# Column maxima brought together on VectorE, one running sum over eight key tiles in the first attention phase, and LayerNorm of the first tiles two ahead of the transposes

## The chip, the cores and the metric

The kernel runs on one core of one Trainium2 chip. The metric is the device time of one execution in microseconds (us), as the median of several runs. Five engines work at the same time, each taking its own instructions strictly in the order in which they were issued: TensorE (PE: matrix products, and transposes by way of an identity matrix; PEld is its loading of weights), VectorE (DVE), ScalarE (ACT), GpSimd (POOL) and SyncE (SP, which here only issues transfers). Semaphores tie them together.

## The reference

One block of a transformer with LayerNorm ahead of each half, in fp32: `x` is [2, 1024, 1024] (batch, tokens, features), there are 32 heads of 32 features, and the hidden width of the second half is 2752.

```python
def attention(x):
    qkv = x @ qkvw + qkvb                      # 1024 -> 3 * 1024
    q, k, v = heads(qkv)                       # [2, 32, 1024, 32] each
    probs = softmax(q @ k.T / sqrt(32))
    return (probs @ v) @ ow + ob

def ffn(x):
    return (silu(x @ W_gate.T) * (x @ W_up.T)) @ W_down.T   # 1024 -> 2752 -> 1024

x = x + attention(layernorm(x))
x = x + ffn(layernorm(x))
```

## The kernel before, in words

**Phases and units.** Attention is done in four phases (2 batches x 2 blocks of 512 queries). A phase has 16 units, and a unit is two heads against 512 queries, that is, 1024 columns. The keys of a unit come in 8 tiles of 128 (`kt` 0 to 7). For each pair of tiles PE computes the transposed scores (`scores`, L510) into two PSUM tiles `s` of 128 keys x 1024 columns; ACT copies each to an SBUF tile `p` (`keep`, L529), and DVE keeps the running maximum over the key tiles in `top` (`largest`, L526).

**The maximum of a column** has then still to be taken over 128 partitions. `maximum` does it in steps that are put off by set delays: two halves, each a transposition of 32x32 blocks on DVE (L549) and a reduction into 16 columns of `part` (L550), at 4600 and 6400 ns; then `turn`, at 10500 ns. In `turn` PE transposes `part` as a whole (L564) into a PSUM tile, and DVE reduces that over its four groups of 32 into `neg`, with the sign changed (L565). `neg` goes to memory at 12000 ns, and comes back spread over all partitions as `m` at 14500 ns (L573).

**Exponentials and sums.** `less_maximum` adds `m` to a tile `p` (POOL, L580; in phase 0 the tiles with `kt % 4 == 3` go to DVE), 3500 ns later ACT takes the exponential (L589), and `add` (L603) adds neighbouring tiles, so that the column of ones that gives the softmax denominator has to be multiplied with fewer tiles. In phase 0 every fourth tile holds the sum of four tiles: tile 1 and tile 5 get one addition, tile 3 and tile 7 two (by 1 and by 2 back). In the other phases every second tile holds the sum of two. `differences` (POOL, L594 and L597) takes differences of the value tiles, so that the products with summed tiles still come out as the plain sum. `values` (L618) multiplies a tile `p` by its values, four products of 32 columns side by side, and, where `summed(kt)` says so, by the ones; in phase 0 that is at `kt` 3 and 7. All of it goes into the PSUM tile `acc`.

**The order of the work** is written out in the program, not found by a scheduler. An `Emitter` merges a list of attention steps (`paced`, one beat per key tile) with a list of other work (`fill`), by a clock that adds up set costs; `later(delay, fn)` puts a step off until that clock has moved on by the delay, and a step can need a mark (`needs=("added", k, kt)`) that another has given. In phase 0, the fill is the projections of q, k (L370) and v (L432) for both batches; in phases 1 to 3 it is output projection (L780), second LayerNorm and feed-forward part of the block before (L922 gate and up products, L1071 down products), and phase 3 is followed by that of the last block alone. On every engine the instructions run in the order in which this merging put them. Projections, transposes, gate, up and down products, and `turn`, all draw their PSUM tile from one pool of three (`lps`); a new tile waits until the tile three before it has been read out. The tiles `p` are a ring of 19.

**The head.** Before phase 0, the first four tiles of 128 tokens are loaded, normed (`norm`, DVE statistics L237 to L246, ACT scaling L247) and transposed on PE (L258) through the same three PSUM tiles, with the read-out of the first half of a tile on DVE (L264) and the second on ACT (L266). `ln_steps` issues the norm of the tile `ahead` places further on before the transposes of the present one; here `ahead` is 1.

Of the kernel before, what the change touches and what calls it, by code (L numbers as in the profile page):

```python
# [9 lines left out]
F32 = mybir.dt.float32  # L10
F32R = mybir.dt.float32r
AF = mybir.ActivationFunctionType
ALU = mybir.AluOpType
AX = mybir.AxisListType

P = 128
HEADS = 32
HD = 32
# [86 lines left out]
def merged(main, side):  # L105

    out, m, n = Steps(), len(main.items), len(side.items)
    for i, step in enumerate(main.items):
        out.items.append(step)
        out.items.extend(side.items[i * n // m : (i + 1) * n // m])  # L110
    return out
# [19 lines left out]
def preln_block_kernel(  # L131
# [14 lines left out]
    nc = tc.nc  # L146
# [3 lines left out]
    NT = S // P  # L150
    NS = S // NH
    NHF = H // NH
    TB = NH // P
# [4 lines left out]
    HPG = P // HD  # L158
# [8 lines left out]
    const = ctx.enter_context(tc.tile_pool(name="const", bufs=1))  # L167
# [29 lines left out]
    def lps(name, shape=(P, NH)):  # L197
        return psum.tile(list(shape), F32, tag="lin", bufs=3, name=name)

    def small(shape, tag, bufs, name):  # L200
        return const.tile(shape, F32, tag=tag, bufs=bufs, name=name)

    ident = const.tile([P, P], F32, tag="ident", name="ident")
# [25 lines left out]
    em = Emitter()  # L229
# [229 lines left out]
    NQ = NH // 2  # L459


    part = const.tile([P, P], F32, tag="part", name="part")
    nc.vector.memset(part, 0.0)

    class Unit:

# [75 lines left out]
        def maximum(self):  # L542

            n = HD // NS
            self.m = att.tile([P, S], F32, tag="m", bufs=2, name=f"m_{self.name}")

            def half(s):
                cols = slice(s * NH, (s + 1) * NH)
                nc.vector.transpose(self.m[:, cols], self.top[:, cols])  # L549
                nc.vector.tensor_reduce(  # L550
                    part[:, s * n : (s + 1) * n],
                    self.m[:, cols].rearrange("p (b j) -> p b j", j=HD),
                    AX.X,
                    ALU.max,
                )

            for s in range(NS):
                em.later(4600.0 + 1800.0 * s, lambda s=s: half(s))
            d2 = dram.tile([S], F32, tag="d2", bufs=3, name=f"d2_{self.name}")
            neg = small([HD, HD], "neg", 1, f"neg_{self.name}")  # L560

            def turn():
                pt = lps(f"top_{self.name}", (P, P))
                nc.tensor.transpose(pt, part, ident)  # L564
                nc.vector.tensor_reduce(  # L565
                    neg, pt[:HD, :].rearrange("b (a i) -> b i a", i=HD), AX.X, ALU.max, negate=True
                )

            em.later(10500.0, turn)
            em.later(12000.0, lambda: nc.sync.dma_start(d2.rearrange("(b i) -> b i", i=HD), neg))  # L570
            em.later(
                14500.0,
                lambda: nc.sync.dma_start(self.m, d2.partition_broadcast(P)),  # L573
                ("max", self.n),
            )

        def less_maximum(self, kt):
            p = self.p[kt]
            eng = nc.vector if self.phase == 0 and kt % 4 == 3 else nc.gpsimd
            eng.tensor_tensor(p, p, self.m, ALU.add)  # L580
            em.later(3500.0, lambda: self.exponential(kt))
            if kt % 2 == 1:
                twice = self.phase == 0 and kt % 4 == 3
                em.later(8100.0, lambda: self.add(kt, 1), None if twice else ("added", self.n, kt))
                if twice:
                    em.later(9900.0, lambda: self.add(kt, 2), ("added", self.n, kt))

        def exponential(self, kt):
            nc.scalar.activation(self.p[kt], self.p[kt], AF.Exp, scale=SCALE)  # L589
# [1 line left out]
        def differences(self):  # L591

            v = self.v.rearrange("p (i a) n -> p i a n", a=2)
            nc.gpsimd.tensor_tensor(v[:, :, 0, :], v[:, :, 0, :], v[:, :, 1, :], ALU.subtract)  # L594
            if self.phase == 0:
                v = self.v.rearrange("p (i a) n -> p i a n", a=4)
                nc.gpsimd.tensor_tensor(v[:, :, 1, :], v[:, :, 1, :], v[:, :, 3, :], ALU.subtract)  # L597

        def add(self, kt, back):


            eng = nc.vector if self.phase == 0 or kt % RUN == RUN - 1 else nc.gpsimd
            eng.tensor_tensor(self.p[kt], self.p[kt], self.p[kt - back], ALU.add)  # L603

        def summed(self, kt):
            return kt % (4 if self.phase == 0 else 2) == (3 if self.phase == 0 else 1)

        def values(self, kt):

# [592 lines left out]
    def joined(qs):  # L1202
        out_ = Steps()
        for k in qs:
            out_.items.extend(k.items)
        return out_

    with tc.manual_schedule():

        head, fill, keep_qk = Steps(), Steps(), Steps()  # L1210

        def two(fn, *args, **kw):

            q = Steps()
            fn(q, *args, **kw)
            return q

        def ln_steps(q, b, t0, t1, tools, ahead):

            load, norm, turn, _ = tools  # L1220
            for t in range(t0, t1):
                if t + ahead < t1:
                    q.add(lambda t=t + ahead: norm(t))
                turn(q, t)
                if t + 5 < NT:
                    q.add(lambda t=t + 5: load(t))

        tools = load, norm, turn, _ = ln1(0)
        for t in range(4):
            head.add(lambda t=t: load(t))  # L1230
        head.add(lambda: nc.sync.dma_start(bqk_t, b_qk))
        for _ in range(4):
            head.add(wst.next)
        head.add(lambda: load(4))
        for _ in range(8):
            head.add(dst.next)
        for _ in range(5):
            head.add(wst.next)
        head.add(lambda: norm(0))
        ln_steps(head, 0, 0, TB, tools, 1)  # L1240
        for _ in range(2):
            head.add(dst.next)
        qk_steps(head, 0, 0, [0])
        head.add(lambda: norm(TB))
        side = two(ln_steps, 0, TB, NT, tools, 1)
        head.items += merged(two(v_steps, 0, 0, range(TB)), side).items
        qk_steps(head, 0, 0, [1])

        v_steps(fill, 0, 0, range(TB, NT))
        for g in range(1, G // 2):  # L1250
            qk_steps(fill, 0, g)
        v_steps(fill, 0, 1)
        for g in range(G // 2, G - 2):
            qk_steps(fill, 0, g)

        tools = load1, norm1, turn1, stats1 = ln1(1)
        for t in range(5):
            fill.add(lambda t=t: load1(t))
        qk_steps(fill, 0, G - 2, [0])
        fill.items += merged(two(qk_steps, 0, G - 1, [0]), stats1(0, TB)).items  # L1260
        last = two(qk_steps, 0, G - 2, [1])
        qk_steps(last, 0, G - 1, [1])
        fill.items += merged(last, two(ln_steps, 1, 0, TB, tools, 1)).items
        fill.items += merged(two(v_steps, 1, 0, range(2)), stats1(TB, TB)).items
        fill.items += merged(
            two(v_steps, 1, 0, range(2, TB)), two(ln_steps, 1, TB, NT, tools, 1)
        ).items
        v_steps(fill, 1, 0, range(TB, NT))
        for g in range(0, G // 2):
            qk_steps(fill, 1, g)  # L1270
        v_steps(fill, 1, 1)
        for g in range(G // 2, G - 2):
            qk_steps(fill, 1, g)
        for s in range(NS):
            for g in range(G - 2, G):
                qk_steps(keep_qk, 1, g, [s])
            if s == 0:
                keep_qk.add(lambda: None, gives=("half", 1))

        def rest(n):  # L1280

            q, late, st = Steps(), Steps(), {}
            b, blk = divmod(n, NS)
            turn = oproj_steps(q, b, blk, st)
            ffn_steps(q, b, blk, st, turn)
            while late.cost < 30 * MM4:
                late.items.insert(0, q.items.pop())
            return q, late


        rests = [rest(n) for n in range(B * NS)]
        lists = attention_steps([(n + 1) * UNITS * NT + 2 * NT for n in range(B * NS - 1)])
        side = [*prep_ctx(0), *prep_ctx(1)]
        em.run(head)
        em.run(fill, lists[0], side=(*side, weight_sum_steps()))
        keep = keep_qk
        for (q, late), beats in zip(rests, [*lists[1:], None]):
            em.run(joined([keep, q]), beats, side=side)
            keep = late
        em.run(keep)  # L1300
        em.settle(True)
# [51 lines left out]
```

## Time and profile before

| | |
|---|---|
| median of 3 runs | 3283.42 us (3279.31 to 3285.41) |
| profiled execution, its own time | 3281.96 us |
| its span, first to last instruction | 3280.2 us |
| mean granted TensorE clock | 0.994 |
| PE busy | 3217.5 us (98%) |
| DVE, ACT, POOL busy | 1920.4, 1431.2, 1758.6 us |
| transposes in `turn` (L564) | 64, together 19.0 us busy |
| reductions in `turn` (L565) | 64, mean 272 ns |
| products with ones (L618) | 1792 instructions, together 137.7 us busy |
| additions of `p` on DVE (L603) | 192, mean 1595 ns |

A line of the profile's list of groups names the source line, the engine, the operation, output and inputs, the shapes, the number of instructions, their busy time together, the mean of one in nanoseconds, and the idle time of the engine just before them with what ended it. Ends of matmuls are modelled, and neighbouring ones overlap, so the busy time of PE is no measure of what an instruction costs there; the distance from one start to the next is. A line of the list of waits names who waited, for whom, the sum in us, the number of times and the longest. Phase 0 lasts from about 120 to 860 us, phase 1 to about 1540, phase 2 to about 2210, phase 3 to about 2770, and the last block's feed-forward part follows.

### The profile page before, as it was taken

How to read it: one execution, taken by the hardware profiler on the slowest of the kernel's cores; microseconds unless marked ns; L12 is line 12 of the kernel's file. 1: busy time of each engine (PE TensorE's matmuls, PEld its weight loads, DVE VectorE, ACT ScalarE, POOL GpSimd, SP SyncE). 2: the span in 40 equal slices, each digit the busy share in tenths (PEclk: the TensorE clock that was granted, in tenths of full speed). 3: DMA queues.
4: the chain of work that ended last, by engine and by line, in shares of the span. 5: the costliest groups of instructions: out<-in, count | busy, mean ns of one | idle time of the engine just before them, and what ended most of it. 6: DMA issues, size and time to landing. Idle time of an engine off the chain costs nothing. (4 is left out here: it accounts for less than half of the span.)

```text
span 3280.2 us, 43732 instructions
## 1 busy us (share of the span) xinstructions
PE 3217.5 (98%) x16320; PEld 1801.1 (55%) x16320; DVE 1920.4 (59%) x2478; ACT 1431.2 (44%) x1570; POOL 1758.6 (54%) x871
## 2 busy tenths in 40 slices
PE   8999999999999999999999999989999999999999
PEld 4444444444347655663466556634655566477775
DVE  2265676666356766666666666676666664344334
ACT  2244554444455545563655455545555554010000
POOL 0267776876676655568665555667765665200000
PEclk9999999999999999999999999999999999999999
DMA  4556766655534445446344444463444444544442
GB/s 155 171 184 193 226 192 203 200 180 161 158 99 135 142 151 146 146 146 200 107 142 145 139 141 137 145 192 110 137 145 146 146 138 140 184 151 153 153 152 97
DMA packets 337826, 507.29 MB, mean 155 GB/s; under 512 B 105424, under 2 KB 122064, under 8 KB 337616
## 3 DMA queue, kind: packets, MB, share of 16 engines
q1 hardware_dynamic: 281424, 405.91, 40.3%
q10 hardware_dynamic: 56192, 98.60, 9.8%
q8 instruction: 130, 2.13, 0.3%
q14 instruction: 80, 0.66, 0.1%
HBM read 429.14 MB, written 75.24 MB: 154 GB/s over the span
## 5 line engine op out<-in xcount | busy, mean ns | idle before, releaser
L580 POOL TENSOR_TENSOR p<-p,m 128x1024 f32<-128x1024 f32 x480 | 1180.8, 2483 | 13.6 <-DMA m<-d 13.4
L529 ACT COPY p<-s 128x1024 f32<-128x1024 f32 x512 | 516.7, 1011 | 872.1 <-DVE top L526 664.5
L526 DVE TENSOR_TENSOR top<-s,top 128x1024 f32<-128x1024 f32 x384 | 468.1, 1219 | 289.0 <-PE s L510 280.0
L589 ACT ACTIVATE p<-p 128x1024 f32<-128x1024 f32 x512 | 532.2, 1057 | 234.7 <-POOL p L580 206.8
L922 PE MATMUL p<-sum,m 128*128 128x256 f32 x2688 | 617.8, 383 | 4.9 <-DVE sum L904 3.3
L603 POOL TENSOR_TENSOR p<-p,p 128x1024 f32<-128x1024 f32 x96 | 227.2, 2367 | 658.9 <-ACT p L589 598.3
L922 PEld LDWEIGHTS p<-sum,m 128*128 128x128 f32 x2688 | 503.2, 190 | 124.7 <-issue 43.0
L922 PE MATMUL p<-xn2T,m 128*128 128x256 f32 x2016 | 473.5, 384 | 1.9 <-ACT gate L934 1.3
L370 PE MATMUL pq<-xnT,wqk 128*128 128x512 f32 x1024 | 463.7, 601 | 0.0
L1071 PE MATMUL pd<-wp,h 128*128 128x512 f32 x960 | 442.3, 607 | 8.3 <-DVE x L1084 6.4
L922 PEld LDWEIGHTS p<-xn2T,m 128*128 128x128 f32 x2016 | 378.2, 191 | 98.5 <-issue 45.4
L603 DVE TENSOR_TENSOR p<-p,p 128x1024 f32<-128x1024 f32 x192 | 306.2, 1595 | 134.1 <-ACT p L589 134.0
L370 PEld LDWEIGHTS pq<-xnT,wqk 128*128 128x128 f32 x1024 | 187.2, 190 | 252.8 <-issue 249.0
L1071 PEld LDWEIGHTS pd<-wp,h 128*128 128x128 f32 x960 | 179.3, 193 | 242.5 <-issue 203.4
L510 PE MATMUL s<-q,k 32*128 32x512 f32 x2048 | 300.8, 645 | 7.1 <-ACT p L529 7.0
L1084 DVE TENSOR_TENSOR x<-pd,x 128x512 f32<-128x512 f32 x360 | 236.9, 681 | 86.8 <-PE pd L1071 86.7
L618 PE MATMUL acc<-p,vals 128*32 128x256 f32 x4096 | 266.0, 383 | 1.8 <-DVE p L603 1.8
L1184 POOL TENSOR_TENSOR ws<-raw 128x512 f32<-128x512 f32 x62 | 93.7, 1512 | 299.9 <-DMA raw<-in_w_gu 170.5
L432 PE MATMUL pvv<-wv,xnT 128*128 128x512 f32 x512 | 233.3, 600 | 1.5 <-ACT xnT L266 1.5
L780 PE MATMUL po<-wo,ctx 128*128 128x512 f32 x512 | 234.6, 607 | 0.0
L618 PEld LDWEIGHTS acc<-p,vals 128*32 128x32 f32 x4096 | 120.1, 110 | 143.6 <-issue 70.2
L950 ACT ACTIVATE gate<-gate 128x512 f32<-128x512 f32 x84 | 52.9, 630 | 278.4 <-DVE gate L949 278.0
(96 smaller groups left out, 2451.3 us busy)
## 6 DMA issues: line engine op xcount, KB each, us to landing
m<-dws SPq DMA_DIRECT2D x336, 256.0 KB
m<-in_w_gu SPq DMA_DIRECT2D x252, 256.0 KB
wp<-ddn SPq DMA_DIRECT2D x160, 256.0 KB
m<-d SPq DMA_DIRECT2D x64, 512.0 KB
wp<-in_w_dn SPq DMA_DIRECT2D x120, 256.0 KB
raw<-in_w_gu ACTq DMA_DIRECT2D x84, 256.0 KB
dws<-ws ACTq DMA_DIRECT2D x84, 256.0 KB
x<-in_x SPq DMA_DIRECT2D x32, 512.0 KB
```

The source lines that it names most:

```text
L370: nc.tensor.matmul(ps, wqk[b, g, w, hk][:, k, :], xnT[b, s][:, kc, :], start=(kc == 0), stop=(kc == KC - 1),)
L510: nc.tensor.matmul(ps[a][:, h * NH : (h + 1) * NH], self.k[rows, i * P : (i + 1) * P], self.q[rows, :], start=True, stop=True,)
L526: nc.vector.tensor_tensor(self.top, s, self.p[0] if kt == 1 else self.top, ALU.max)
L529: nc.scalar.copy(self.p[kt], s)
L580: eng.tensor_tensor(p, p, self.m, ALU.add)
L589: nc.scalar.activation(self.p[kt], self.p[kt], AF.Exp, scale=SCALE)
L603: eng.tensor_tensor(self.p[kt], self.p[kt], self.p[kt - back], ALU.add)
L618: nc.tensor.matmul(self.acc[j * HD : (j + 1) * HD, c : c + NQ], w(h), self.p[kt][:, q0 : q0 + NQ], start=start, stop=stop, skip_group_chec ...
L780: nc.tensor.matmul(st["ps"], ctxT[b, blk][:, g, t * P : (t + 1) * P], st["w"][hf, g], start=(g == 0), stop=(g == G - 1),)
L922: nc.tensor.matmul(ps, mats[c, n][:, kc, :], rhs, start=(kc == 0), stop=(kc == hk - 1),)
L1071: nc.tensor.matmul(st["pd"], lefts[n](pi)[:, j, t * P : (t + 1) * P], st["wp", pi, n, j], start=(j == 0), stop=(j == PART // 2 - 1),)
L1084: nc.vector.tensor_tensor(xs, st["pd"], xs, op)
```

## The change

Three things are changed. `turn` no longer uses PE and PSUM: `part` has 32 columns instead of 128, DVE transposes each of its four 32x32 blocks into `turned` and reduces that; `turn` is due at 8200 instead of 10500 ns. In phase 0 tile 7 gets a third addition (4 back), so that it holds the sum of all eight tiles; the ones are multiplied with tile 7 alone, and POOL takes one more difference of values per unit. In the head, tile 1 is normed before the first transposes, and from there on the norms run two tiles ahead.

```diff
-    part = const.tile([P, P], F32, tag="part", name="part")
-    nc.vector.memset(part, 0.0)
+    part = const.tile([P, HD], F32, tag="part", name="part")
...
+            turned = small([HD, HPG, HD], "turned", 1, f"turned_{self.name}")
             def turn():
-                pt = lps(f"top_{self.name}", (P, P))
-                nc.tensor.transpose(pt, part, ident)
+                for a in range(HPG):
+                    nc.vector.transpose(turned[:, a, :], part[a * HD : (a + 1) * HD, :])
                 nc.vector.tensor_reduce(
-                    neg, pt[:HD, :].rearrange("b (a i) -> b i a", i=HD), AX.X, ALU.max, negate=True
+                    neg, turned.rearrange("b a i -> b i a"), AX.X, ALU.max, negate=True
                 )
-            em.later(10500.0, turn)
+            em.later(8200.0, turn)
...
             if kt % 2 == 1:
-                twice = self.phase == 0 and kt % 4 == 3
-                em.later(8100.0, lambda: self.add(kt, 1), None if twice else ("added", self.n, kt))
-                if twice:
-                    em.later(9900.0, lambda: self.add(kt, 2), ("added", self.n, kt))
+                backs = [b for b in (1, 2, 4) if self.phase == 0 and (kt + 1) % (2 * b) == 0] or [1]
+                for i, back in enumerate(backs):
+                    em.later(
+                        8100.0 + 1800.0 * i,
+                        lambda back=back: self.add(kt, back),
+                        ("added", self.n, kt) if back == backs[-1] else None,
+                    )
...
             if self.phase == 0:
                 v = self.v.rearrange("p (i a) n -> p i a n", a=4)
                 nc.gpsimd.tensor_tensor(v[:, :, 1, :], v[:, :, 1, :], v[:, :, 3, :], ALU.subtract)
+                v = self.v
+                nc.gpsimd.tensor_tensor(v[:, 3, :], v[:, 3, :], v[:, 7, :], ALU.subtract)
...
         def summed(self, kt):
-            return kt % (4 if self.phase == 0 else 2) == (3 if self.phase == 0 else 1)
+            n = NT if self.phase == 0 else 2
+            return kt % n == n - 1
...
         head.add(lambda: norm(0))
-        ln_steps(head, 0, 0, TB, tools, 1)
+        head.add(lambda: norm(1))
+        ln_steps(head, 0, 0, TB, tools, 2)
```

## The prediction

> **What bounds the kernel now.** I read the page's busy times first, then PE's list of waits, the groups by shape, the granted clock around the longest waits, and the timeline at two places.
>
> ```profile
> PE 3217.5 (98%) x16320; PEld 1801.1 (55%) x16320; DVE 1920.4 (59%) x2478; ACT 1431.2 (44%) x1570; POOL 1758.6 (54%) x871
> ```
>
> PE is hardly ever idle, so the time is PE's work plus PE's few waits. What leaves PE counts almost in full; what is put on another engine counts only where PE comes to wait for it. The waits, us in sum, times, longest:
>
> ```profile
> PE top L564 <- DVE part L550: 16.1, 10, 3.0
> PE pt_a L258 <- ACT x L247: 10.2, 4, 7.8
> PE pd L1071 <- DVE x L1084: 7.1, 12, 1.4
> PE s L510 <- ACT p L529: 7.0, 5, 2.6
> ...
> PE top L564 <- DVE xn2T L264: 2.0, 1, 2.0
> PE acc L618 <- DVE p L603: 1.8, 2, 1.5
> ```
>
> The longest entry is the transpose that the change removes: PE reaches it before DVE has reduced `part`, and everything queued on PE behind it stands still. The second entry is the head. The groups that change:
>
> ```profile
> L603 DVE TENSOR_TENSOR p<-p,p 128x1024 f32<-128x1024 f32 x192 | 306.2, 1595 | 134.1 <-ACT p L589 134.0
> ...
> L618 PE MATMUL acc<-p,ones 128*32 128x256 f32 x1792 | 137.7, 379 | 0.0
> ...
> L549 DVE STREAM_TRANSPOSE m<-top 128x512 f32<-128x512 f32 x128 | 89.9, 702 | 1.8
> ...
> L564 PE MATMUL top<-ident,part 128*128 128x128 f32 x64 | 19.0, 297 | 19.0 <-DVE part L550 16.1 <-DVE xn2T L264 2.0 <-DVE x L1084 0.7
> ...
> L565 DVE TENSOR_REDUCE neg<-top 32x32 f32<-32x128 f32 x64 | 17.4, 272 | 38.6 <-PE top L564 38.4
> ```
>
> DVE in turn stood 38.4 us waiting for these transposes. Around one of the long waits (columns: stretch, length, busy of PE, PEld, DVE, ACT, POOL, granted clock, DMA):
>
> ```profile
> 2028.10:2030.80 2.70, 0.02 (x4) 0.00 (x0) 2.67 (x6) 1.01 (x1) 0.00 (x0) 1.00 0.33 97
> ...
> 2032.95:2036.36 3.41, 3.41 (x5) 1.30 (x4) 2.95 (x6) 0.00 (x0) 0.00 (x0) 0.50 0.36 100
> 2036.36:2040.00 3.64, 3.64 (x51) 1.65 (x49) 1.70 (x2) 2.54 (x3) 0.50 (x1) 1.00 0.37 122
> ```
>
> PE idles 2.7 us, and soon after the granted clock is 0.50 for 3.41 us. So a long wait costs twice.
>
> **The compiled order.** The change leaves the order of all other instructions on PE as it was, but for shifts by one product in some places. The sum can therefore be made instruction by instruction, against the profiled execution's 3281.96 us.
>
> **A, the transposes' own time.** Start to next start, a transpose amid products takes 0.109 us (49 of 64), right after scores 0.165 us (15): 5.3 + 2.5 = 7.8 us gained.
>
> **B, the waits ahead of them.** The list has 19.0 us for L564; from start to start it is 21.6 us, since modelled ends hide some 0.17 us of each. What is late next decides how much stays. At 1531 and 2200 (2.5 and 2.9 us) scores and then 6.9 us of output projection follow, which need no read-out by DVE for long: gained in full, likewise the 2.0 us at 1612. At 1820, 1947 and 2030 (2.1, 1.8, 2.8 us) down products follow. There two `pd` tiles wait for DVE, and `top` took the slot of the first; without it the next `pd` takes that slot, free at 2029.43 after the first read-out instead of 2031.96 after the second, and the one behind takes the second's. Some 2 of the 2.8 us stay. At 979 (3.1 us) DVE is busy without a break (norm 2.54, halves, an addition, sums), and the gate product waits for the same sums as before: I keep 1.3. The other nine together have 4.4 us. This is some 18 us; DVE's new work takes about 3 of it back, so 15. Ends: 8 (new work and evictions eat half) and 21.6.
>
> **New work on DVE.** Four transposes of 32x32 and a reduction per unit. No row shows such a transpose: below it is bounded by 0.059 us (the smallest DVE row, a 128x1 memset), above by the 0.70 us of 128x512. Rows with few columns take 0.16 to 0.21 (reciprocal 128x1, aggregate 128x2), the nearest, so 0.19: 0.76 us per unit, 49 us in all on an engine with 1360 us to spare. The reduction replaces one of 0.27 us. They wait for DVE alone, directly after the second half, and the 38.4 us of waiting for PE goes. Queued behind them are an addition of `p` and read-outs of `pd`, for which PE waits; that is the 3 us above. The transfer of `neg` on SP's queue is due at the same 12000 ns, with `neg` never later; I count nothing for it.
>
> **C, the clock.** Half-speed stretches of 6.83 us (at 981.6) and 3.41 us (1534.6, 1821.3, 1947.6, 2032.9, 2203.6) follow six of these waits, of 1.8 to 3.1 us. At half speed they cost half their length, 11.95 us. I count the five short ones: 8.5 us; ends 1.7 and 12.
>
> The page TensorE: Matmul & The Clock Gate of the Trainium skill (Part 1) says that the clock is halved after at least one idle window of about 3.4 us. None of these waits is that long, so by that rule C would be 0 and the time 8.5 us longer; the rows show the halving after shorter ones.
>
> **D, the ones.** In phase 0 the 256 passes with ones take 17.44 us from start to next start. Half go: 8.7 us.
>
> **E, the third addition.** The products of tile 7 now wait for it, and behind them on PE stand the ones and all projections. The chain at one of 16 units:
>
> ```profile
> 192.11 1.14 PE L510 MATMUL s<-q,k 32*128 32x512 f32 x8
> 193.18 3.70 PE L370 MATMUL pq<-xnT,wqk 128*128 128x512 f32 x8
> 193.28 1.22 DVE L526 TENSOR_TENSOR top<-s,top 128x1024 f32<-128x1024 f32 x1 [2.42 <-PE s L510]
> 194.43 2.19 DVE L603 TENSOR_TENSOR p<-p,p 128x1024 f32<-128x1024 f32 x1
> 196.53 1.21 DVE L526 TENSOR_TENSOR top<-s,top 128x1024 f32<-128x1024 f32 x1
> 196.81 1.93 PE L618 MATMUL acc<-p,vals 128*32 128x256 f32 x32
> ```
>
> DVE takes two maxima and an addition after the scores; the third addition is queued behind the second maximum. It starts at 197.66 and with 1.22 us ends at 198.88, while tile 7's products, the last eight passes of the 32, start at 198.13: 0.75 us of waiting. I did this for each unit: at 1.22 us the waits are 0.75, 0.37, 1.95, 2.2, 0.67 and 0.6 us in six units and none in ten, 6.5 us. In phase 0, 67 of 97 such additions take 1.20 to 1.42 us and the others up to 3.23; at 2.2 us each the sum is 17.9. Weighted 2 to 1, 10 us. Two of the waits exceed 1.9 us, so one halving of the clock, 1.7 us: 12 in all; ends 6.5 and 23.
>
> The page SBUF — State Buffer (section SBUF: two separate sides) says that a DVE operation with two SBUF inputs is shut out for the whole of a GpSimd operation that holds the shared ports. Were each third addition to meet a whole POOL addition of 2.48 us, it would take 3.70 us, E would be about 44 us and the change 4 us slower; the row's longest is 3.23 and two thirds show no delay.
>
> POOL's further difference takes at most the 0.78 us of the row twice its size, 16 times, in a phase where POOL is busy 512 of 740 us; the sums of tiles 0 to 3 end 1.5 us or more ahead of their products, which covers it. Uncovered it would cost 12.5 us.
>
> **F, the head.** Tile 2's statistics move ahead of the read-out of tile 0, tile 2's and 3's norms come about 1 us earlier, but their transposes then wait for the three PSUM slots, read out later. Followed through with the durations there, the first projection starts at 17.5 instead of 17.98 us: 0.5 gained (-1 to 1.5).
>
> **Sum.** 7.8 + 15 + 8.5 + 8.7 - 12 + 0.5 = 28.5 us; 3281.96 - 28.5 = 3253.5. The median of the runs is 1.46 above the profiled execution: 3255.
>
> **Rivals.** *The waits move.* Read-outs are late wherever `part` was, and PE stops a little further on: B 5, C 2, gain 12, 3271. For: in the window at 2028 DVE is busy 2.67 of 2.70 us. Against: slots come free earlier, and after 1531 and 2200 nothing is to be read out. *All of it goes and the additions fit:* B 21.6, C 12, E 6.5, gain 44, 3239. *The additions cost what all else brings:* E 23, B 8, C 1.7, F -1: gain 2, 3281. *VectorE sets phases 1 to 3 (slower):* if a 32x32 transpose costs nearly what 128x512 does, 2.0 us more per unit than assumed stand ahead of read-outs that PE waits for; in 48 units 98 us, less 28, 3353. It decides where four transposes cost 0.7 us a unit more than assumed, 0.37 us each. Against: transposes and reductions of 128x512 take about 1 ns a column, so 32 columns can't take as long unless the fixed part is nearly all of it.
>
> **Chances.** What a measurement can tell from no change is 0.2%, 6.6 us. Forecast 0.55 (own range 3243 to 3267), waits move 0.18, all goes 0.15, additions 0.07, VectorE 0.05. Faster: 0.55 + 0.15 + most of 0.18 = 0.83; same 0.11; slower 0.06. The range from 3238 to 3277 leaves out the lower end of "all goes", the upper part of "waits move" and the last two.
>
> **What would show it.** Right: no PE wait over 1.5 us where the transposes stood after 1500 us, half-speed stretches down to about four, PE waits of some 10 us on the additions of `p` in phase 0, a 32-column transpose near 0.19 us. Wrong: PE's wait for `pd` read-outs well over 7.1 us (the waits moved), or for additions over 20 us.

## The result, and the profile after

The changed kernel takes 3300.94 us (median of 12 runs) where the kernel before takes 3283.61 in the same comparison: 1.0053 of the time, with a 95% interval of 1.0039 to 1.0067. It is some 17 us slower; 28.5 us faster was forecast. The profiled execution has a span of 3297.6 us, against 3280.2.

The page's line of busy times (engine, busy us, share of the span, instructions):

```profile
PE 3213.4 (97%) x16128; PEld 1791.1 (54%) x16128; DVE 2047.3 (62%) x2749; ACT 1432.6 (43%) x1570; POOL 1784.3 (54%) x887
```

PE has 192 instructions fewer, 64 transposes and 128 passes with ones, so that part of the forecast came about. Yet the span grew, so PE must wait more. Its list of waits says for whom:

```profile
PE acc L627 <- DVE p L611: 31.4, 17, 4.9
PE pd L1080 <- DVE x L1093: 11.5, 15, 1.9
PE s L509 <- ACT p L528: 11.4, 8, 3.6
PE pt_a L258 <- ACT x L247: 8.0, 2, 7.8
PE pvv L432 <- ACT xnT L266: 3.8, 1, 3.8
...
PE p L931 <- DVE sum L840: 2.4, 1, 2.4
```

The 19 us at the transposes are gone. The products `acc` now wait 31.4 us for the additions of `p` instead of 1.8 (19.1 of them in phase 0, 18.0 of these at the products of tile 7), and read-outs of `pd` and copies of the scores hold PE for longer than before. The groups that answer to those shown of before:

```profile
L611 DVE TENSOR_TENSOR p<-p,p 128x1024 f32<-128x1024 f32 x208 | 383.4, 1844 | 107.1 <-ACT p L595 106.5
...
L627 PE MATMUL acc<-p,ones 128*32 128x256 f32 x1664 | 130.4, 385 | 0.0
...
L548 DVE STREAM_TRANSPOSE m<-top 128x512 f32<-128x512 f32 x128 | 89.9, 702 | 1.8
...
L566 DVE STREAM_TRANSPOSE turned<-part 32x32 f32<-32x32 f32 x256 | 50.9, 199 | 3.5
...
L567 DVE TENSOR_REDUCE neg<-turned 32x32 f32<-32x128 f32 x64 | 23.4, 365 | 2.2
```

A small transpose takes 0.199 us, as assumed, and the reduction 0.365 instead of 0.272. The additions went from a mean of 1595 ns to 1844, though only 16 were added to 192: those that were there before became longer too.

The timeline at the fourth unit of phase 0, a place for which the prediction had no wait (start, length, engine and line; "x3" are three in a row):

```profile
315.88 1.14 PE L509 MATMUL s<-q,k 32*128 32x512 f32 x8
316.95 4.56 PE L370 MATMUL pq<-xnT,wqk 128*128 128x512 f32 x10
317.05 1.23 DVE L525 TENSOR_TENSOR top<-s,top 128x1024 f32<-128x1024 f32 x1 [5.50 <-PE s L509]
318.19 1.22 DVE L611 TENSOR_TENSOR p<-p,p 128x1024 f32<-128x1024 f32 x1
...
319.32 1.22 DVE L525 TENSOR_TENSOR top<-s,top 128x1024 f32<-128x1024 f32 x1
320.46 7.17 DVE L611 TENSOR_TENSOR p<-p,p 128x1024 f32<-128x1024 f32 x3
320.99 3.34 POOL L582 TENSOR_TENSOR p<-p,m 128x1024 f32<-128x1024 f32 x1
321.44 1.50 PE L627 MATMUL acc<-p,vals 128*32 128x256 f32 x24
324.28 2.26 POOL L1193 TENSOR_TENSOR ws<-ws,raw 128x512 f32<-128x512 f32 x1
325.46 0.64 PE L627 MATMUL acc<-p,vals 128*32 128x256 f32 x8 [2.52 <-DVE p L611]
```

The same place in the timeline of the kernel before:

```profile
311.35 1.22 DVE L603 TENSOR_TENSOR p<-p,p 128x1024 f32<-128x1024 f32 x1 [3.95 <-ACT p L589]
311.89 1.14 PE L510 MATMUL s<-q,k 32*128 32x512 f32 x8
...
313.06 1.23 DVE L526 TENSOR_TENSOR top<-s,top 128x1024 f32<-128x1024 f32 x1 [0.49 <-PE s L510]
314.21 1.21 DVE L603 TENSOR_TENSOR p<-p,p 128x1024 f32<-128x1024 f32 x1
315.34 1.22 DVE L526 TENSOR_TENSOR top<-s,top 128x1024 f32<-128x1024 f32 x1
```

There the addition of tile 6 to tile 7 ran ahead of the first maximum, at 311.35, while the scores were not there yet, and only one addition lay between the two maxima. In the changed kernel that same addition stands behind the first maximum (318.19), since VectorE's instructions come in another order. The three additions in a row from 320.46 are the one 2 back (1.65 us), the third one, which takes 3.26 us while GpSimd adds (320.99 to 324.33), and the first of the next unit. PE does the 24 passes of tiles 4 to 6 and stands from 322.9 to 325.46, when the third addition is done. What follows on the clock (columns as before):

```profile
322.50:325.50 3.00, 0.48 (x13) 0.04 (x7) 2.96 (x2) 1.06 (x1) 3.00 (x2) 1.00 0.23 83
...
326.90:330.30 3.40, 3.40 (x5) 1.35 (x4) 0.72 (x1) 0.28 (x1) 3.40 (x2) 0.50 0.77 237
330.40:333.00 2.60, 2.60 (x13) 0.84 (x12) 0.90 (x1) 1.06 (x1) 2.60 (x3) 1.00 0.13 42
```

A wait of 2.5 us, and 1.4 us later 3.4 us at half clock. Before, phase 0 had no such stretch; now it has six, 23.9 us long. PE stands for 2.5 us of them anyway, and the rest costs half its length, some 11 us. By the starts of the scores, phase 0 loses 26.6 us and the later phases bring some 9 back.

### The profile page after: what moved, and what is told of

It reads as the page before. It is cut to its first block, busy times and chain, and to the rows that moved or that the text cites. A ratio compares the mean times of both kernels' runs of the same rounds, so it can differ in the third digit from the quotient of the medians.

```text
span 3297.6 us, 43645 instructions
## 1 busy us (share of the span) xinstructions
PE 3213.4 (97%) x16128; PEld 1791.1 (54%) x16128; DVE 2047.3 (62%) x2749; ACT 1432.6 (43%) x1570; POOL 1784.3 (54%) x887
## 4 chain that ended last, share of the span: by engine, by line
PE 84%; DVE 8%; DMA 3%; issue 2%; POOL 2%; ACT 2%; SPq 0%; ACTq 0%; POOLq 0%; DVEq 0%
PE p L931 31%; PE pq L370 12%; PE pd L1080 11%; PE acc L627 9%; PE s L509 7%; PE pvv L432 6%; PE po L789 5%; DVE top L525 2%; DVE p L611 2%; PE pd L1007 1%; DVE x L1093 1%; POOL p L582 1%; PE pg L975 1%; DMA ctx<-dctx 1%; DMA rec<-drec 1%
## 5 line engine op out<-in xcount | busy, mean ns | idle before, releaser
L582 POOL TENSOR_TENSOR p<-p,m 128x1024 f32<-128x1024 f32 x480 | 1193.2, 2508 | 12.2 <-DMA m<-d 12.2
L611 DVE TENSOR_TENSOR p<-p,p 128x1024 f32<-128x1024 f32 x208 | 383.4, 1844 | 107.1 <-ACT p L595 106.5
L627 PE MATMUL acc<-p,vals 128*32 128x256 f32 x4096 | 272.1, 385 | 31.5 <-DVE p L611 31.4
```

Source lines behind the costliest of these rows:

```text
L627: nc.tensor.matmul(self.acc[j * HD : (j + 1) * HD, c : c + NQ], w(h), self.p[kt][:, q0 : q0 + NQ], start=start, stop=stop, skip_group_chec ...
```

## The experiments

Theory 1: the third addition in phase 0, and PE's waits for it, are what makes the change slow. Theory 2: it is VectorE's new work for the maxima, ahead of all that is queued behind it.

**The parts one by one.** e1 has only the `turn` part of the diff, e2 only the sums of eight (`add`, `summed`, the further difference), e3 only the head, e4 `turn` and the head:

```diff
 # e1, in turn():
-                nc.tensor.transpose(pt, part, ident)
+                for a in range(HPG):
+                    nc.vector.transpose(turned[:, a, :], part[a * HD : (a + 1) * HD, :])
 # e2, in less_maximum():
+                backs = [b for b in (1, 2, 4) if self.phase == 0 and (kt + 1) % (2 * b) == 0] or [1]
 # e3, in the head:
+        head.add(lambda: norm(1))
+        ln_steps(head, 0, 0, TB, tools, 2)
```

> Only the maxima are brought together on VectorE; the sums of four and the head are as before. Theory 1 (the third addition in phase 0 is what makes the change slow): 8 to 15 us faster than before, since the 64 transposes and their waits go and phase 0 is undisturbed; PE's wait for additions of p in phase 0 stays under 2 us. Theory 2 (the new work of VectorE pushes all that is queued behind it): 0 to 15 us slower, with PE waits for additions and pd read-outs above those of before in phases 1 to 3.

> Only the sums of eight in phase 0; maxima on TensorE and the head are as before. Theory 1: 20 to 35 us slower than before, all of it in phase 0 (the 16th unit's scores some 27 us later), with PE waiting about 20 us on the additions of p and several stretches of half clock in phase 0. Theory 2: within 10 us of before, as sums of eight alone gain 8.7 us and wait for some 6 us.

> Only the norms of the head's first tiles two ahead. Both theories: within 2 us of before; the first projection starts between 17 and 18 us.

> The change without the sums of eight. Theory 1: the sum of the two parts alone, 8 to 16 us faster than before. Theory 2: 0 to 15 us slower than before.

| kernel | us | ratio to before, 95% interval |
|---|---|---|
| e1, maxima on VectorE | 3270.23 | 0.9965 (0.9951 to 0.9978) |
| e2, sums of eight | 3305.87 | 1.0076 (1.0059 to 1.0093) |
| e3, head | 3281.0 | 1.0001 (0.999 to 1.0012) |
| e4, maxima and head | 3270.39 | 0.9966 (0.9956 to 0.9977) |

The sums of eight cost 25 us, the maxima gain 11.5, the head does nothing that can be measured. The parts add to some 13.5 us slower, near the 17 of the whole. In e2 PE waits 18.9 us for additions in phase 0, and there are six stretches of half clock there:

```profile
PE acc L624 <- DVE p L608: 18.9, 11, 2.9
```

Theory 1 holds, theory 2 falls as the cause of the loss. Both e1 and e4 are faster than either kernel of the case. The waits of e1, however, are hardly shorter in sum than before, 56.3 us against 58.6:

```profile
PE s L509 <- ACT p L528: 11.3, 8, 3.6
PE pd L1072 <- DVE x L1085: 10.8, 16, 1.9
...
PE acc L619 <- DVE p L604: 7.9, 5, 2.7
```

Before, these three were 7.0, 7.1 and 1.8. The 14 us more, and some 6 us at other places (2.3 at two `sum`, 2.2 at `xnT`, 1 at `gate`), take the place of the 19 us at the transposes. The profiled execution of e1 is the slowest of its six, but that of e4, which lies at its median, has 10.4, 11.9 and 9.4 at the same three places. How much of the waits for additions is the maxima's stays open: in e3, where only the head differs, they are 6.8 us, with one of 4.3.

**What in the sums of eight costs.** e5 lets VectorE do the third addition, but into a tile that nothing reads:

```diff
+            out_ = self.p[kt - back] if back == 4 else self.p[kt]
-            eng.tensor_tensor(self.p[kt], self.p[kt], self.p[kt - back], ALU.add)
+            eng.tensor_tensor(out_, self.p[kt], self.p[kt - back], ALU.add)
```

> The kernel with the sums of eight alone, but the third addition writes over tile 3, which nothing reads any more, so that the products of tile 7 do not wait for it; VectorE and GpSimd do the same work. (The softmax sums therefore leave out tiles 0 to 3.) Waiting theory (PE's waits at tile 7 and the half clock behind them are the cost): 4 to 9 us faster than before, no waits for additions in phase 0. Load theory (the additions and GpSimd hold each other up, and that delays other things PE needs): 8 us or more slower than before.

Measured: 3284.14 us, 0.9998 of before (0.9988 to 1.0009). Between the two expectations. Without the wait at tile 7 the 25 us of e2 are gone, and with them the waits for additions in phase 0 (0.9 us). But the kernel is no faster than before beyond the noise, though the passes with ones take 8.7 us less from start to next start (17.4 to 8.7 in the 16 units). So the additions, with GpSimd's further difference, cost some 8 us even where no product waits for them (by the interval, 5 to 12). The waits of phase 0 in the profiled execution show where that may lie:

```profile
PE s L510 <- ACT p L529: 3.7, 2, 2.5
PE top L564 <- DVE part L550: 1.9, 1, 1.9
PE pt_a L258 <- ACT qk L384: 1.9, 1, 1.9
PE acc L625 <- DVE p L609: 0.9, 1, 0.9
```

None of the first three exceeded 1.0 us in phase 0 before; two stretches of half clock, 10.2 us in all, come with them. This is one execution of each kernel, and such waits differ among kernels without sums of eight as well: the third is 0.3 us in e3 and 2.5 in e9.

**Ways round the wait.** e6 adds tile 3's sum into tile 4, when tile 4 is due, so that tile 7 keeps two additions:

```diff
+            if self.phase == 0 and kt == 4:
+                em.later(8100.0, lambda: self.add(kt, 1))
...
+            nc.gpsimd.tensor_tensor(w[:, 3, :], w[:, 3, :], w[:, 4, :], ALU.subtract)
```

> Sums of eight, with the fourth step moved: tile 3's sum is added into tile 4 (due with tile 4, some 15 us earlier) instead of into tile 7, so that tile 7 has two additions as before; GpSimd takes five smaller differences instead of two. The same number of additions on VectorE. Waiting theory: 4 to 9 us faster than before. Load theory: slower than before by 5 us or more.

Measured: 3288.9 us, 1.0017 (1.0005 to 1.0029), some 6 us slower, as the load theory had it. The waits at `acc` in phase 0 are down to 2.6 us, but `pt_a` waits 4.5 us for ACT's read-out and the scores 4.5 us for ACT's copies, in a profiled execution that is 7.7 us above the median. e8 is e6 with maxima and head:

> Maxima on VectorE, head two ahead, and the sums of eight with the step into tile 4. Waiting theory: both gains together, 14 to 20 us faster than before. Load theory: no better than the maxima alone, which were 11.5 us faster, or worse.

Measured: 3274.01 us, 0.9968 (0.9954 to 0.9981), no better than e4 without any sums of eight, again as the load theory had it. e7 keeps the third addition but issues the products later, with nine projections between scores and products instead of four:

```diff
+                if backs[-1] == 4:
+                    em.later(last + 5000.0, lambda: None, ("added", self.n, kt))
```

> Sums of eight as in the change, but the products of tiles 4 to 7 are issued some five projections later on PE, so that 9 instead of 4 projections lie between scores and products. Waiting theory: 2 to 9 us faster than before, waits for additions in phase 0 under 4 us. Load theory: slower than before.

Measured: 3293.31 us, 1.0029 (1.0018 to 1.004); a miss for the waiting theory. At tile 7 the wait is gone in all 16 units. But PE still waits 12.4 us for additions in phase 0, where 4 were expected, all of it at the products of tile 3 in eight units. The later products changed VectorE's order too: in 14 of the 16 units a maximum now stands between tile 3's two additions, in e2 in none. So e7 moved the wait to another tile, and it does not tell what sums of eight cost without one.

**VectorE's work for the maxima.** e9 is e1 with `turn` due at 10500 ns again; e10 is e1 with each small transpose issued twice:

```diff
 # e9
-            em.later(8200.0, turn)
+            em.later(10500.0, turn)
 # e10
-                for a in range(HPG):
+                for a in [*range(HPG), *range(HPG)]:
```

> The maxima on VectorE alone, but due at 10500 ns as in the kernel before, so that VectorE's new work stands behind the additions and read-outs that were queued ahead of the reduction. If the early place of the new work ahead of them is what turned the gain into new waits: 4 us or more faster than the maxima alone at 8200 (more than 15 us faster than before). If VectorE is late in these places anyway: within 4 us of the maxima alone, 8 to 15 us faster than before.

> The maxima on VectorE alone, with the four small transposes issued twice: some 0.8 us more of VectorE per unit, nothing else. If each us of VectorE there is paid by PE: about 40 us slower than the maxima alone. If only the places with waits pay (some 17): 5 to 15 us slower. If the length of this work hardly matters: within 4 us.

e9: 3268.76 us, 0.9949 (0.9934 to 0.9963), the fastest of all and 5 us ahead of e1, but its interval overlaps e1's, so whether the later place is better stays open. e10: 3284.38 us, 1.0001 (0.999 to 1.0012), 12 us slower than e1 (6 to 18 by the two intervals). The group shows what was added:

```profile
L565 DVE STREAM_TRANSPOSE turned<-part 32x32 f32<-32x32 f32 x512 | 102.2, 200 | 14.9
```

51 us more on VectorE cost 12 us: PE pays about a quarter of such work here, though VectorE is busy for no more than 62% of the span.

**GpSimd's part.** In e11 and e12 the additions for sums of weights, which run through phase 0 on GpSimd, are fills of the same tiles; e11 is otherwise the kernel before, e12 the sums of eight alone.

```diff
-                nc.gpsimd.tensor_tensor(out_, in0, in1, op)
+                nc.gpsimd.memset(out_, 0.01)
```

> The kernel before with GpSimd's additions for the sums of weights in phase 0 replaced by fills of the same tiles (the feed-forward products therefore use a constant for the sums of weights). Only a base for the next run: within 5 us of before; VectorE's additions in phase 0 with a mean below 1.5 us.

> The sums of eight alone, with the same replacement on GpSimd. If collisions with GpSimd's operations are what stretches the chain ahead of tile 7: no more than 10 us slower than the run with the light GpSimd and sums of four, and additions in phase 0 of 1.5 us or less. If the chain on VectorE is too long in any case: 15 to 25 us slower, as with the full GpSimd.

e11: 3279.66 us, 0.9983 (0.9974 to 0.9992); additions in phase 0 have a mean of 1.55 us, hardly less than the 1.59 of before and not below 1.5. e12: 3296.28 us, 1.0034 (1.002 to 1.0048). With the light GpSimd the sums of eight cost 16.7 us, with the full one 25, each give or take some 5.5. The waits at `acc` in phase 0 are as long (18.6 against 18.9 us). So these operations are a part of it at most. But the additions are hardly shorter for it either (a mean of 1.68 us in phase 0, 1.77 in e2), so the runs do not tell a long chain on VectorE from one that the remaining GpSimd additions of `m` stretch.

## Why the prediction was wrong, point by point

**E, the third addition, is the step that failed.** Forecast: 12 us, of which 10 for waits and 1.7 for the clock. Measured from start to start, the products of tile 7 wait 20.2 us in 12 of the 16 units. In the six units for which the step, with additions of 1.22 us, had waits they come to 10.4 us; that this is the forecast sum is luck, for one of them has 4.34 us where the step had 1.95, and another 0.18 where it had 0.75. The excess is above all three others, the third, fourth and eleventh unit, with 2.59, 2.70 and 2.63 us where the step had none. These are the three in which VectorE's order changed close to tile 7: the addition of tile 6 to tile 7 moved from ahead of the maximum of tile 4's scores of the next unit to behind it, as the two timelines show for the fourth unit. The step compared the order of the two kernels on PE, took VectorE's chain from the kernel before and hung one addition on its end; e2, the sums of eight alone, has the same move in the same units. The moved addition takes 1.60, 1.22 and 1.64 us there, and the third ones 2.17, 3.26 and 2.17 instead of 1.22. No run puts the old order back, so the share of the move is read from the traces and not shown by a run.

And the clock: two waits over 1.9 us were assumed to bring one halving; six reached 1.4 us or more. Of the six half-speed stretches in phase 0, four come with such waits, one with the wait at `xnT`, and one (at 586.3) after waits of 0.9 us and less; after two of the long waits (1.46 and 2.63 us) the clock stayed whole. The stretches cost some 11 us instead of 1.7. Taking the wait away (e5 against e2) gains 25.6 us (19 to 32 by the two intervals), twice the forecast of 12. The upper end I gave, 23, was near; the value chosen was not.

**The additions' load was left out.** E priced only the wait at tile 7. e5 shows some 8 us without it, e6 with its sixteen additions elsewhere some 14. With it E is some 34 us (the 25 of e2 and the 8.7 that D brings), and D's gain is lost.

**B, the waits ahead of the transposes, was mis-sized too.** A, B and C together were to bring 31 us; e1 brings 11.5. The rival "the waits move" was the right one here: it had 14.8 us for the three. I took 3 us for VectorE's new work; e10 puts a work of that size, on top of the first, at 12 us. C: half-speed stretches after phase 0 (without the one at the very end) went from 41.0 to 30.7 us in e1, a gain of 5 us, less some 3 for a new one in phase 0. Of the 46 us between forecast and result, E has some 22, and A to C have 20; but A to C still brought a gain, and E made a loss of it.

**Right:** the small transposes at 0.199 us against 0.19; D, the passes with ones, with 8.7 us in e5 as forecast; the head, where the first projection starts at 17.11 us (17.5 forecast) and nothing comes of it in the end; the order of instructions on PE; and the rival that VectorE's transposes would cost as much as long ones, which fell. Both signs of being wrong came about: 11.5 us of waits for `pd` read-outs and 31.4 for additions.

**The rules weighed.** The page SBUF — State Buffer of the Trainium skill (SBUF: two separate sides) spoke against the change, and the estimate that the prediction worked out from it, 44 us for E, was nearer to the measured 34 than my 12. But it was not nearer for its reason: it had every third addition meet a whole GpSimd addition and take 3.70 us, and the sixteen took 1.21 to 3.26 us, nine of them 1.22 or less. The clock rule of TensorE: Matmul & The Clock Gate (Part 1), which asks for an idle window of about 3.4 us, disagrees with the rows: here a wait of 2.5 us was followed by half clock.

## What to carry to other kernels

Where PE is busy for 98%, work taken from it counts only if what replaces it is not at the end of a chain that PE meets a few hundred nanoseconds later; read from the trace the time between the last step of that chain and its first reader, unit by unit, and in the order of the changed kernel on every engine of the chain, not only on the one that bounds; price the added step over the whole spread of its group's durations, here 1.21 to 3.26 us. An engine busy for 60% is not free either: 51 us of evenly spread work on VectorE cost 12. Try the parts of a change one by one: here one part lost twice what another gained.

## What was not expected of the hardware

A single VectorE addition of `p` took 10.02 us where it alone takes 1.21, in the output projection's part of phase 1 of the changed kernel:

```profile
942.89 2.52 POOL L781 TENSOR_TENSOR x<-x,bo 128x512 f32<-128x512 f32 x2
...
943.54 10.02 DVE L611 TENSOR_TENSOR p<-p,p 128x1024 f32<-128x1024 f32 x1
...
945.34 2.36 POOL L582 TENSOR_TENSOR p<-p,m 128x1024 f32<-128x1024 f32 x1
...
947.64 2.50 POOL L781 TENSOR_TENSOR x<-x,bo 128x512 f32<-128x512 f32 x2
950.04 1.07 PE L627 MATMUL acc<-p,vals 128*32 128x256 f32 x16
950.08 2.39 POOL L582 TENSOR_TENSOR p<-p,m 128x1024 f32<-128x1024 f32 x1
```

GpSimd runs without a gap from 942.89 to 952.47, and the addition ends 1.1 us after it. At 953.61 PE had waited 1.63 us for it. The longest in the profiled execution of the kernel before is 3.44 us; additions of 9.9 to 10.6 us are also in those of e3, e4, e5, e8, e9 and e11. Since e3 changes only the head and e11 only GpSimd's work, neither the maxima nor the sums of eight are needed for it. Each of the seven ends 1.08 or 1.09 us after the last of a series of GpSimd operations without a gap. So it is not one GpSimd operation that such an addition waits for, but all that follow back to back. Not every series does this: the third addition at 322.14 in the fourth unit ended 1.1 us after the GpSimd addition that ran when it began, though the next one followed at once. What makes the difference stays open.
